# The last chunk's rows of the first sample go straight into y, and y lies in the filters' place

## The chip, the cores and the metric

The kernel runs on one core of one Trainium2 chip. The metric is the device time of one execution in microseconds (us); lower is better. TensorE is called PE, VectorE DVE, ScalarE ACT, GpSimd POOL and SyncE SP, as in the profile. SP does no arithmetic here: it issues DMA transfers, in its program's order, and an issue that waits for a semaphore holds up all issues behind it. POOL and ACT can issue transfers too.

## What is computed

Two layers of a network on x of shape (16, 128, 32, 32): 16 samples, 128 channels, 1024 places. Each layer is a mixer and a feed-forward part, both with a residual. What matters here is the feed-forward part of the first layer and what follows it:

```python
x = x + _L0_conv_ref(_ln_c(x), ...)          # linear attention
t = _to_tokens(x)
t = t + _L0_ffn_ref(_ln_t(t), ...)           # spectral filters: long causal convolutions by FFT,
x = _from_tokens(t, x)                       #   16 filters, two signs, a 128x128 matrix for each
x = x + _L1_conv_ref(_ln_c(x), ...)          # two 3x3 convolutions with batch norm and ReLU
t = _to_tokens(x)
t = t + _L1_ffn_ref(_ln_t(t), ...)           # 64 experts, each token block routed
x = _from_tokens(t, x)
```

The long convolution is a product in the frequency domain: a transform of each sample, at each frequency a product with a 128x128 matrix that is summed over the filters, and an inverse transform.

## The kernel before

It has three stages that follow each other, and the change lies where the second hands over to the third.

**Stage 1, attention and forward transform** (to about 378 us). Sample by sample; the spectra go to DRAM (`vd`), the samples to DRAM (`xd`). DVE mixes the filters' matrices into `mst` (16 KB in each partition), in pieces of 8 of 32 rows.

**Stage 2, products by frequency** (378 to 653 us). The frequencies are cut into `NCH` = 16 chunks of `P / NCH` = 8 rows. For chunk c, PE forms the matrices (`generate`, L816, from `mst` and `ph`), DVE and ACT copy them (`collect`, L827 and L829), and PE multiplies all 16 samples by them (`multiply`, L840). `combine` (L869, L870) and `finish` (L854 to L857) put the results into `ys`, whose partitions are (row in a group of 4, real or imaginary part, sample), so that one chunk of one sample lies in a few partitions only. `finish` then stores `ys` to DRAM as `yd` with two transfers of 512 KB (L861, on SP). The rows of the last two chunks, 14 and 15, have a tensor of their own, `yd[1]` of 16 rows; the other 112 rows are `yd[0]`. `finish` of chunk 15 runs on DVE, of the others on POOL.

**Stage 3, inverse transform, convolutions and routing** (from 653 us; the experts from about 1130 us). `load(b)` (L1032, L1035) fetches sample b: `xd[b]` into `xp`, 512 KB, and its frequencies into `y`, which has two buffers: 112 rows of `yd[0]` (896 KB) and 16 rows of `yd[1]` (128 KB). For sample 0, `xp` and the 112 rows come on POOL's queue, the 16 rows on SP's; for all others everything comes on SP's queue. POOL (L1048 to L1057) and DVE (L1061 to L1078) form `z` from `y`, PE multiplies both with `wi` (L1132, the inverse transform), DVE adds the sample (L1139), and so on through the first convolution: ACT copies the image (L1182, L1189), DVE forms `abss` (L1198), POOL writes `v` from it (L1202), and PE convolves (L1012).

The order of stage 3 on PE, DVE, ACT, POOL and SP is written out ahead of time by a planner that interleaves samples; each engine runs its instructions strictly in that order. At its start the samples 0, 1 and 2 overlap: on DVE and POOL the `z` of sample 2 stands ahead of the first convolution's `abss` and `v` of sample 0. The tensors of the convolution weights (`cw`, twice 1152 KB) and small biases are loaded on SP between sample 1 and sample 2. Each transfer on SP uses one of eight semaphores in turn, so it also waits for the transfer eight before it on those.

So that PE doesn't stand still during the handover, `keep(ps, "cv", 26)` puts 26 products on it whose results nobody reads (L164; each is recorded as two matmuls).

Buffers of a stage lie where those of the stage before lay. `mst` is in the pool `lconst`, which ends with stage 2; the `y` buffers are in the pool `first` of stage 3.

Of the kernel before, what the change touches and what calls it, by code (L numbers as in the profile page):

```python
# [8 lines left out]
F32 = mybir.dt.float32  # L9
AF = mybir.ActivationFunctionType  # L10
ALU = mybir.AluOpType
# [3 lines left out]
P = 128  # L15
B, C, H, W = 16, 128, 32, 32
# [15 lines left out]
NM = NQ // 2  # L32
NCH = 16
JL = 8
# [6 lines left out]
RG = P // KR  # L41
EPR = P // RG
MB = 8
# [26 lines left out]
def metaformer_kernel(ctx: ExitStack, tc: tile.TileContext, io: dict, out: bass.AP):  # L70
    nc = tc.nc
    xs = io["x"].rearrange("b c h w -> b c (h w)")
    outs = out.rearrange("b c h w -> b c (h w)")

    const = ctx.enter_context(tc.tile_pool(name="const", bufs=1))


    ident = const.tile([P, P], F32, name="ident")
# [97 lines left out]
    with ExitStack() as l0:  # L176
        lconst = l0.enter_context(tc.tile_pool(name="lconst", bufs=1))
# [35 lines left out]
            nc.vector.tensor_tensor(seg[:, i : i + 1], seg[:, i - 1 : i], hard[:, i : i + 1], ALU.add)  # L213
        coef = lconst.tile([P, NF], F32, name="coef")
        nc.vector.tensor_scalar(coef, wmix, sig, None, ALU.mult)
        mst = lconst.tile([P, EPR, C], F32, name="mst")
        ph = lconst.tile([P, NCH, CW], F32, name="ph")


        with ExitStack() as a0:  # L220
# [427 lines left out]
            def filters():  # L648

                wfm = setup.tile([P, NQ // 2, 2 * P], F32, name="wfm", tag="mi")  # L650
                nc.vector.tensor_scalar(wfm, wf[:, 1::2, :], -1.0, None, ALU.mult)

                def values(q, dst):
                    for sgn in range(2):
                        w = wfm[:, q // 2, :] if sgn and q % 2 else wf[:, q, :]
                        nc.tensor.matmul(
                            dst, phi[:, q, sgn, :], w, start=(sgn == 0), stop=(sgn == 1)
                        )

                yield  # L660
                xf = spectrum_tile()
                for parity in range(2):
                    pe = class_values(parity, values)
                    t = class_copy(pe, 1)
                    ts = class_copy(pe, ROT) if parity else t
                    ab = class_sums(parity, pe, t)
                    class_differences(parity, ab, pe, ts)
                    yield
                    for part in range(2):
                        butterflies(ab, xf, parity, part)  # L670
                    if parity:
                        butterflies(ab, xf, 1, butterflies(ab, xf, 1, 2))
                    yield
                half = CW // 2
                e, o = (xf[:, :, i].rearrange("p c r m j -> p c (r m j)") for i in range(2))
                nc.vector.tensor_tensor(ph[:, :, :half], e, o, ALU.add)
                nc.vector.tensor_tensor(ph[:, :, half:], e, o, ALU.subtract)
                for m in range(EPR // MB):
                    es = slice(m * MB, (m + 1) * MB)
                    for i in range(NF):  # L680
                        mi = setup.tile([P, MB, C], F32, name="mi", tag="mi")
                        nc.sync.dma_start(mi, io["M_phi"][i, :, es, :])
                        yield
                        if i == 0:
                            nc.vector.tensor_scalar(mst[:, es, :], mi, coef[:, 0:1], None, ALU.mult)
                        else:
                            nc.vector.scalar_tensor_tensor(
                                mst[:, es, :], mi, coef[:, i : i + 1], mst[:, es, :], ALU.mult, ALU.add
                            )

            def prepare():
# [84 lines left out]
        with ExitStack() as g0:  # L776
# [33 lines left out]
            def generate(c, q):  # L810

                pg = [psg.tile([P, 4, CW], F32, name="pg", tag="p") for r in range(RG)]
                for i in range(4):
                    for r in range(RG):
                        rs = slice(r * KR, (r + 1) * KR)
                        nc.tensor.matmul(  # L816
                            pg[r][:, i], mst[rs, 4 * q + i, :], ph[rs, c, :], start=True, stop=True,
                        )
                return pg

# [28 lines left out]
            def finish(c, ys):  # L849

                eng = nc.gpsimd if c + 1 < NCH else nc.vector
                e = cpl.tile([P, JL // RG, 2, C], F32, name="ye", tag="ye", bufs=1)
                yv = ys[:, :, 0]
                eng.tensor_tensor(e, yv[:, :, :2], yv[:, :, 2:], ALU.add)  # L854
                eng.tensor_tensor(yv[:, :, 2:], yv[:, :, :2], yv[:, :, 2:], ALU.subtract)
                eng.tensor_tensor(yv[:, :, 0], e[:, :, 0], e[:, :, 1], ALU.add)
                eng.tensor_tensor(yv[:, :, 1], e[:, :, 0], e[:, :, 1], ALU.subtract)  # L857
                for kl in range(JL // RG):
                    last = c + 2 >= NCH
                    j0 = kl * RG + (c - NCH + 2 if last else c) * JL  # L860
                    nc.sync.dma_start(  # L861
                        yd[last][j0 : j0 + RG].rearrange("g r b x e -> (g r b) (x e)"),
                        ys[:, kl].rearrange("p x m e -> p (x m e)"),
                    )
# [69 lines left out]
    with ExitStack() as c1:  # L934
# [11 lines left out]
        RING = tuple(f"xp{pr}" for pr in AWAY) + (  # L946
            "y", "wi", "z", "y", "cw0", "v", "cw1", "p1", "yo",
        )
        FIRST = ("wi", "v", "cw0", "cw1", "p1", "y")
        halves = {}  # L950

        def load_half(h):

# [2 lines left out]
            if g >= E // EG:  # L956
                pr = AWAY[0] + h - 2 * (E // EG)
                if pr in AWAY:
                    tag = RING[(pr - AWAY[0] + 18) % len(RING)]
                    pool = first if tag in FIRST else xpool if tag[:2] == "xp" else work  # L960
                    x = pool.tile([P, 2, N], F32, name=f"xb{pr}", tag=tag, bufs=RING.count(tag))
                    for j in range(2):
                        xt[2 * pr + j] = x[:, j]
                        nc.sync.dma_start(x[:, j], xd[2 * pr + j])
                return
            pool = first if tag in FIRST else xpool if tag[:2] == "xp" else work
            w = pool.tile([P, EG * HID], F32, name=f"we{n}", tag=tag, bufs=RING.count(tag))
            if n == 0:
                nc.sync.dma_start(
# [53 lines left out]
        def tokens(t):  # L1023
            return t.rearrange("p (j c) -> p j c", c=C)

        yts, xp = {}, {}

        def load(b):
            if b % 2 == 0:
                xp[b // 2] = xpool.tile([P, 2, N], F32, name=f"xp{b // 2}", tag=f"xp{b // 2}")  # L1030
            xt[b] = xp[b // 2][:, b % 2]
            (nc.sync if b else nc.gpsimd).dma_start(xt[b], xd[b])  # L1032
            yts[b] = first.tile([P, 2, 2 * NM, C], F32, name="y", tag="y", bufs=2)
            for i, js in enumerate((slice(P - 2 * JL), slice(P - 2 * JL, P))):
                (nc.gpsimd if b + i == 0 else nc.sync).dma_start(  # L1035
                    yts[b][js].rearrange("p r x e -> p r (x e)"),
                    yd[i][:, :, b].rearrange("j r x e -> j r (x e)"),
                )


# [456 lines left out]
        with tc.manual_schedule(engines=PINNED | {mybir.EngineType.SP}):  # L1497
# [7 lines left out]
            for j in range(2):  # L1505
                nc.sync.dma_start(b2[j * E : (j + 1) * E, :], w2[:, HID, :])
            samples = [None] * B
            keep(ps, "cv", 26)
            for b, name in order:
                if name == "yin":  # L1510
                    if b > 1:
# [303 lines left out]
```

## Time and profile before

| | us |
|---|---|
| median of 4 runs | 1238.72 (1237.3 to 1244.49) |
| the profiled execution, its own time | 1238.84 |
| its span, first to last instruction | 1237.0 |
| outside the span | 1.84 |
| PE busy in the span | 1162.1 (94%) |
| DVE, ACT, POOL busy | 934.5, 724.9, 603.4 |
| mean granted clock of PE | 0.992 of full speed |

By stretches of the span (busy us of each engine, DMA as the mean busy share of the 16 DMA engines):

| stretch, us | PE | DVE | ACT | POOL | clock | DMA |
|---|---|---|---|---|---|---|
| 396 to 640, stage 2 | 239.44 of 244 | 176.23 | 185.41 | 202.64 | 1.00 | 0.38 |
| 640 to 665, handover | 21.07 of 25 | 8.11 | 3.45 | 9.52 | 0.97 | 0.66 |
| 665 to 700, start of stage 3 | 28.46 of 35 | 20.77 | 12.54 | 12.15 | 0.87 | 0.75 |
| 700 to 1130, stage 3 | 415.83 of 430 | 376.20 | 229.09 | 160.08 | 1.00 | 0.31 |
| 1130 to 1237, experts and output | 91.59 of 107 | 41.59 | 23.96 | 9.44 | 0.95 | 0.90 |

PE's busy time in the handover counts the products of `keep`, so it is not all work. A row of the chain of waits gives start, duration and the step; it is followed back from the last instruction, so work on it is work that something later waited for. In the timeline the brackets at the end of a row give the idle time of the engine before it and who ended that.

### The profile page before, as it was taken

The numbers are of one execution on the slowest core, as the hardware profiler recorded it, in microseconds if no ns is written. First come the engines' busy times: TensorE is split into PE (matmuls) and PEld (weight loads), VectorE is DVE, ScalarE is ACT, GpSimd is POOL, SyncE is SP. The second block draws the span as 40 slices with busy tenths as digits, with TensorE's granted clock in tenths as the row PEclk, the third lists the DMA queues.
The fourth block names the chain that finished last, engine by engine and source line by source line (L and its number), as shares of the span: only waits on it lengthen the run. The fifth ranks groups of instructions, "written<-read, shape, count | busy, mean of one in ns | idle before, by whom it ended". The sixth has DMA issues, their size and how long they took to land.

```text
span 1237.0 us, 34413 instructions
## 1 busy us (share of the span) xinstructions
PE 1162.1 (94%) x14398; PEld 954.8 (77%) x14398; DVE 934.5 (76%) x1944; ACT 724.9 (59%) x1420; POOL 603.4 (49%) x800
## 2 busy tenths in 40 slices
PE   7889999999999999999997899999999999998996
PEld 6667777777767998888887788898888888885453
DVE  5888888888766777777764589898988989885235
ACT  4777787777655777777761345555555555544211
POOL 2435454655568788888882433343343333230003
PEclk9999999999999999999998999999999999999998
DMA  7005334353436334343449522223233321416899
GB/s 281 24 31 168 120 116 154 96 171 101 154 120 180 103 126 139 133 139 132 131 135 288 127 51 52 86 87 120 84 122 118 103 86 69 154 34 223 317 403 384
DMA packets 91243, 175.14 MB, mean 142 GB/s; under 512 B 5968, under 2 KB 42064, under 8 KB 90448
## 3 DMA queue, kind: packets, MB, share of 16 engines
q1 hardware_dynamic: 90448, 170.46, 41.3%
q0 software_dynamic: 640, 2.49, 0.6%
q8 instruction: 113, 1.85, 0.6%
q14 instruction: 42, 0.34, 0.1%
HBM read 110.28 MB, written 62.65 MB: 140 GB/s over the span
## 4 chain that ended last, share of the span: by engine, by line
PE 55%; DVE 22%; issue 11%; ACT 6%; DMA 4%; POOL 1%; SPq 1%; POOLq 0%; ACTq 0%; DVEq 0%
PE pg L816 10%; PE pcv L1012 10%; PE py L840 9%; PE big L638 7%; DVE bst L135 4%; PE big L171 3%; PE big L152 3%; PE big L570 3%; PE big L450 2%; PE big L533 2%; PE big L432 2%; DVE abss L1255 1%; DVE xp L1277 1%; DVE xp L1139 1%; ACT tt L144 1%
## 5 line engine op out<-in xcount | busy, mean ns | idle before, releaser
L1012 PE MATMUL pcv<-v,cw 128*128 128x256 f32 x1152 | 259.9, 382 | 3.5 <-POOL v L1202 3.5
L1012 PEld LDWEIGHTS pcv<-v,cw 128*128 128x128 f32 x1152 | 216.1, 191 | 36.9 <-issue 4.9
L829 ACT COPY g<-pg 128x512 f32<-128x512 f32 x316 | 161.2, 606 | 39.2 <-PE pg L816 38.6
L827 DVE COPY g<-pg 128x512 f32<-128x512 f32 x196 | 127.8, 682 | 70.4 <-PE pg L816 70.4
L816 PE MATMUL pg<-ph,mst 32*128 32x128 f32 x4096 | 144.1, 280 | 5.8 <-issue 4.5
L816 PEld LDWEIGHTS pg<-ph,mst 32*128 32x128 f32 x4096 | 128.6, 186 | 22.2 <-issue 11.8
L840 PE MATMUL py<-g,v 128*32 128x128 f32 x4096 | 124.7, 274 | 1.3 <-POOL v L808 1.3
L840 PEld LDWEIGHTS py<-g,v 128*32 128x32 f32 x4096 | 108.0, 110 | 9.1 <-POOL v L808 1.8
L144 ACT ACTIVATE tok<-tok,sts 128x128 f32<-128x128 f32 x256 | 101.9, 480 | 16.9 <-DVE sts L1089 13.6
L135 DVE BATCH_NORM_STATS2 bst<-big 128x6 f32<-128x256 f32 x256 | 91.2, 418 | 21.1 <-PE big L152 11.7
L807 POOL TENSOR_TENSOR v<-xc 128x256 f32<-128x256 f32 x128 | 99.6, 801 | 13.6 <-DMA xc<-vd 13.3
L638 PE MATMUL big<-u,mu 128*128 128x128 f32 (+4 forms) x384 | 86.0, 380 | 0.0
L1202 POOL TENSOR_TENSOR v<-abss 128x256 f32<-128x256 f32 x64 | 49.1, 787 | 68.1 <-DVE abss L1198 56.7
L286 POOL TENSOR_TENSOR xf<-ab 128x256 f32<-128x256 f32 x34 | 24.8, 728 | 110.4 <-DVE ab L253 110.3
L1221 POOL TENSOR_TENSOR yo<-abss 128x256 f32<-128x256 f32 x32 | 23.5, 734 | 110.3 <-DVE abss L1217 110.3
L638 PEld LDWEIGHTS big<-u,mu 128*128 128x128 f32 x384 | 56.8, 191 | 18.0 <-issue 15.4
L570 PE MATMUL big<-wf,ub 128*128 128x256 f32 x256 | 62.0, 385 | 0.2
L144 ACT ACTIVATE tt<-tt,sts 128x128 f32<-128x128 f32 x128 | 51.1, 481 | 14.6 <-DVE sts L1089 14.6
L808 POOL TENSOR_SCALAR v<-v 128x256 f32<-128x256 f32 x64 | 55.2, 863 | 5.6
L475 POOL TENSOR_TENSOR ke<-ke,ks 128x1024 f32<-128x1024 f32 x16 | 30.6, 1913 | 55.1 <-DVE qs L483 43.5
L570 PEld LDWEIGHTS big<-wf,ub 128*128 128x128 f32 x256 | 46.2, 190 | 8.7 <-ACT xn L423 3.0
L914 ACT COPY yt<-py 128x512 f32<-128x512 f32 x60 | 35.1, 585 | 28.0 <-ACT g L829 18.0
(256 smaller groups left out, 2488.6 us busy)
## 6 DMA issues: line engine op xcount, KB each, us to landing
we<-in_weight SPq DMA_DIRECT2D x32, 1024.0 KB, 9.2
xc<-vd SPq DMA_DIRECT2D x64, 256.0 KB, 3.3
yd<-ys SPq DMA_DIRECT2D x32, 512.0 KB, 3.5
vd<-xf SPq DMA_DIRECT2D x15, 1024.0 KB, 5.1
y<-yd SPq DMA_DIRECT2D x15, 896.0 KB, 6.6
x<-in_x SPq DMA_DIRECT2D x16, 512.0 KB, 5.0
mi<-in_M_phi SPq DMA_DIRECT2D x16, 512.0 KB, 4.6
xd<-x SPq DMA_DIRECT2D x16, 512.0 KB, 6.3
```

Source lines behind the costliest of these rows:

```text
L135: nc.vector.bn_stats(bst[:, j : j + 2, :].rearrange("p j s -> p (j s)"), src[:, j : j + 2, :].rearrange("p j c -> p c j"),)
L144: nc.scalar.activation(dst[:, j, :], src[:, j, :], AF.Identity, bias=nm[:, j : j + 1], scale=r[:, j : j + 1],)
L570: nc.tensor.matmul(dst, self.ub[:, q, :], wf[:, q, :], start=True, stop=True)
L638: nc.tensor.matmul(self.pa[:, a:hi], mu[:, NF - 1 - si, tap, :], self.u[:, a - tap : hi - tap], start=(tap == 0), stop=(tap == KU - 1),)
L807: nc.gpsimd.tensor_tensor(vv[:, x, 1:, bs], e, o, op)
L808: nc.gpsimd.tensor_scalar(v[:, :, 0, bs], v[:, :, 2, bs], -1.0, None, ALU.mult)
L816: nc.tensor.matmul(pg[r][:, i], mst[rs, 4 * q + i, :], ph[rs, c, :], start=True, stop=True,)
L827: nc.vector.tensor_copy(dst, src)
L829: nc.scalar.copy(dst, src)
L840: nc.tensor.matmul(py[rows, x, kl, :], v[:, (x * NM + m) * JL + jl, 1 - ri : 3 - ri, :] .rearrange("p k b -> p (k b)"), g[:, ((x * 2 + ri) ...
L1012: nc.tensor.matmul(pc[:, i], wt[:, dy, k, :], v[:, k, dy * WT : dy * WT + HT], start=(dy == 0), stop=(dy == 2),)
L1202: nc.gpsimd.tensor_tensor(v[:, k, WT : WT + HT], self.ab[:, 0], self.ab[:, 1], op)
```

## The change

Three things, in the text below with the parts that only follow from them left out.

- **A short way for 8 of sample 0's rows.** `finish` of chunk 15 first copies sample 0's part of `ys` straight into `y` of sample 0: four transfers from SBUF to SBUF, each of 4 partitions and 16 KB, two issued by SP and two by ACT. Only then it issues its two stores to `yd`. `load(0)` now fetches 112 rows and the 8 rows of chunk 14, both on POOL's queue. `load(1)` and later fetch 112 and 16 rows on SP as before.
- **`y` in the filters' place.** A new pool, `ypool`, lies outside all stages and has two buffers of 8 KB in each partition under the tag "y". In stages 1 and 2 they hold `mst`, now two tiles of 16 rows each; in stage 3 they hold `y`. The pool `first` no longer holds `y`, so its other tiles lie at other addresses.
- **A shorter stopgap on PE.** `keep(ps, "cv", 26)` becomes `keep(ps, "cv", 13)`.

```diff
+    ypool = ctx.enter_context(tc.tile_pool(name="ypool", bufs=2, reuse_waits="tile"))
+    def y_tile(b):
+        if b not in yts:
+            yts[b] = ypool.tile([P, 2, 2 * NM, C], F32, name="y", tag="y", bufs=2)
+        return yts[b]
...
-        mst = lconst.tile([P, EPR, C], F32, name="mst")
+        mst = [
+            ypool.tile([P, EPR // 2, C], F32, name=f"mst{i}", tag="y", bufs=2) for i in range(2)
+        ]
+        def mrow(i, n=1):
+            h, k = divmod(i, EPR // 2)
+            return mst[h][:, k : k + n]
...
                 eng.tensor_tensor(yv[:, :, 1], e[:, :, 0], e[:, :, 1], ALU.subtract)
+                for kl in range(JL // RG if c + 1 == NCH else 0):
+                    for r in range(2):
+                        j0 = P - JL + kl * RG
+                        (nc.scalar if kl else nc.sync).dma_start(
+                            y_tile(0)[j0 : j0 + RG, r].rearrange("p x e -> p (x e)"),
+                            ys[r * B :: 2 * B, kl].rearrange("p x m e -> p (x m e)"),
+                        )
                 for kl in range(JL // RG):
                     last = c + 2 >= NCH
...
             (nc.sync if b else nc.gpsimd).dma_start(xt[b], xd[b])
-            yts[b] = first.tile([P, 2, 2 * NM, C], F32, name="y", tag="y", bufs=2)
-            for i, js in enumerate((slice(P - 2 * JL), slice(P - 2 * JL, P))):
-                (nc.gpsimd if b + i == 0 else nc.sync).dma_start(
-                    yts[b][js].rearrange("p r x e -> p r (x e)"),
-                    yd[i][:, :, b].rearrange("j r x e -> j r (x e)"),
+            n = JL if b else 0
+            for i, js in enumerate((slice(P - 2 * JL), slice(P - 2 * JL, P - JL + n))):
+                (nc.sync if b else nc.gpsimd).dma_start(
+                    y_tile(b)[js].rearrange("p r x e -> p r (x e)"),
+                    yd[i][: js.stop - (js.start or 0), :, b].rearrange("j r x e -> j r (x e)"),
                 )
...
-            keep(ps, "cv", 26)
+            keep(ps, "cv", 13)
```

With the planner's order unchanged, the order of instructions on each engine differs only here: SP issues two small transfers between the stores of chunk 14 and those of chunk 15, and no longer one of 16 rows behind them; ACT issues two small transfers after its last copy of stage 2; POOL issues one more load, of 8 rows, behind the 112; PE has 13 products fewer. The filters' products are the same, from two tiles.

## The prediction

> **What bounds the kernel now.** I read the busy time by stretches first. The change can only act where stage 2 hands over to stage 3, so I then took the chain of waits there; its lines from 652 to 691 us are these.
>
> ```profile
> 652.54 0.34 DVE ys L857
> ...
> 652.90 0.32 SPq L861
> ...
> 653.27 6.98 DMA yd<-ys
> ...
> 660.69 0.63 SPq L1035
> ...
> 663.27 10.31 DMA cw<-cwd
> ...
> 673.59 12.18 DMA y<-yd
> ...
> 685.87 0.43 DVE z L1061
> ...
> 688.89 0.61 DVE abss L1198
> ...
> 689.56 0.73 POOL v L1202
> ```
>
> The chain is not what one expects. It goes from the last result (DVE, 652.88) to its store, which lands at 660.24, to SP's row of issues from 660.69 on, and then not through sample 0 at all: it stays in the DMA queue, through `cw` and the load of `y` of sample 2, which lands at 685.8. Only there does it return to an engine. In the timeline this is seen from the engines' side.
>
> ```profile
> 664.18 0.43 DVE L1061 TENSOR_TENSOR z<-y 128x256 f32<-128x256 f32 x1 [11.30 <-DMA y<-yd]
> ...
> 683.02 1.02 ACT L1189 COPY p<-big 128x1024 f32<-128x1024 f32 x1
> ...
> 685.87 0.43 DVE L1061 TENSOR_TENSOR z<-y 128x256 f32<-128x256 f32 x1 [5.94 <-DMA y<-yd]
> ```
>
> DVE waits 11.30 us for `y` of sample 0 and later 5.94 us for `y` of sample 2. Behind the second wait stands `abss` of sample 0 (688.81), whose input, ACT's copy L1189, was done at 684.04. So sample 0 was ready 4.77 us before it could go on: a head start of sample 0 alone would only lengthen that wait. What sets the end here is when the DMA queue reaches `y` of sample 2. The table by stretches of 2 us shows that queue (the last two columns are DMA share and GB/s; ahead of them the granted clock).
>
> ```profile
> 654.00:656.00 2.00, 2.00 (x12) 1.74 (x11) 0.00 (x0) 0.00 (x0) 0.00 (x0) 1.00 1.04 330
> 656.00:658.00 2.00, 2.00 (x11) 1.77 (x10) 0.00 (x0) 0.00 (x0) 0.00 (x0) 1.00 1.01 393
> 658.00:660.00 2.00, 2.00 (x11) 1.77 (x10) 0.00 (x0) 0.00 (x0) 0.00 (x0) 1.00 0.48 197
> 660.00:662.00 2.00, 0.91 (x5) 0.46 (x3) 0.00 (x0) 0.00 (x0) 0.00 (x0) 1.00 0.01 4
> 662.00:664.00 2.00, 0.00 (x0) 0.00 (x0) 0.00 (x0) 0.00 (x0) 0.00 (x0) 0.89 0.69 238
> 664.00:666.00 2.00, 1.67 (x8) 1.70 (x9) 1.78 (x3) 0.00 (x0) 1.75 (x2) 0.50 1.03 342
> ```
>
> The DMA engines are full to 658, all but empty to 662.6, and full again to 690. They are empty because SP stands still from 653.7 to 660.69: its next issue, the last 16 rows of sample 0, waits for the store, and everything for the later samples stands behind it.
>
> **The change, part by part.** The sum is made against the profiled execution, 1238.84 us (span 1237.0 and 1.84 outside), 0.12 above the median.
>
> First, sample 0. Removed is the way over DRAM: store (landed 660.24), issue 0.63, landing 3.4 us after the issue, 664.1. Added are four transfers of 16 KB from 652.9 on. An issue of SP on such tiles took 0.32 to 0.44 us (the four stores, L861), so SP's second leaves at about 653.3 and ACT's likewise. Nothing in the trace is an SBUF to SBUF transfer; the smallest there, `gb` with 0.2 KB, landed after 2.4 us, the 128 KB load after 3.4. That puts them at 655.7 to 656.7. The later bound for `y` of sample 0 is POOL's queue: the 112 rows, issued at 648.36, landed after 9.9 us, 658.3. The 8 rows of chunk 14 wait for that chunk's stores (issued 647.83, landing 5.1 later, 652.9), are 64 KB, and come behind the 112 rows; I put `y` at 658.6. Its bounds: 658.3, and 662.8 if the 8 rows take the 9.9 us of their predecessor from 652.9. Sample 0 then starts 5.5 us earlier (1.3 in the slow case). On POOL only `z` stands behind the added issue, which takes about 0.7 us (the 112-row issue, 0.69); on ACT, idle for 25.49 us until 675.46, nothing does.
>
> The Trainium skill speaks against splitting: DMA: Bandwidth & Descriptors, Bandwidth, asks for about 1 MiB a transfer and calls those under 64 KB dominated by descriptors. By that page's fit (Anatomy of one DMA), about 2.0 us fixed for each, an estimate of mine for two on one queue without any overlap is 4.0 us, which the sum would not feel.
>
> Second, SP's queue, where the gain is. No wait for the store remains ahead of sample 1's `xp` and its 112 rows: they need only chunk 14's stores (652.9), so they are issued from about 654.3, against 661.38 and 661.99. The stores of chunk 15 go out some 0.7 us later (two issues), but the DMA engines are busy then with POOL's loads. The wait for the last store (about 660.9) now stands ahead of sample 1's 16 rows; `cw`, the biases and sample 2 are queued behind it. At that time most of sample 1's 1.4 MB still lies in the queue, at 300 GB/s (between the rows' 289 and 342 at 664 to 668) up to 4.7 us of work, so it doesn't run dry before `cw` follows. What is saved is the empty time: (1 - 0.48) x 2 + (1 - 0.01) x 2 + (1 - 0.69) x 2 = 3.64 us. A second hole, 668 to 670 with a share of 0.88, comes from the same late start (SP waits for sample 1's landing until 670.70) and gives 0.24. Bytes don't change: 4 x 16 KB and 64 KB for 128 KB. `y` of sample 2 lands 3.9 us earlier, 681.9. Its other conditions are met: its buffer is free when POOL has read sample 0, 667.78 - 5.5 = 662.3, and its queue slot when sample 1's last rows have landed, about 667.
>
> Third, what is late next. `z` of sample 2 ends 2.9 us after its landing (685.87 to 688.81), at 684.9; sample 0's input is ready at 684.04 - 5.5 = 678.5, or 682.7 in the slow case. Sample 1's `y` lands at about 671.0 - 3.9 = 667.1 (its last rows, issued at 662.62, took 8.4), where `z` of it would like to start at 671.47 - 5.5 = 666.0; that costs sample 0 about 1 us of a slack of 6. So the whole 3.9 goes on to `abss`, `v` and PE's convolution (690.34 to 686.4). From there the trace has no wait for a load of `y`: the queue is empty at 691 and SP waits for DVE, 44.7 us in all to 760. So the shift is kept; the expert weights at the end are issued behind computed results and move along.
>
> Fourth, PE's stopgap: 13 fewer products, 26 matmuls of 11.49 / 52 = 0.221 us, end at 655.2 for 660.9. PE idles from there to `y`, about 3.4 us; before it was 3.42 (660.91 to 664.33), and the clock was 0.50 from 664 to 670. I expect the same clock. If the cover is gone and the clock falls sooner, sample 0's first products run slow as they do now, under the same slack: nothing. Products of no use don't set the end.
>
> A rule from the skill belongs here: TensorE: Matmul & The Clock Gate, What's actually happening, has the clock halved after an idle window of about 3.4 us that runs freely, so a gap of this length may or may not fall. By the rule sample 0 may run at full clock, which the sum again doesn't feel.
>
> Fifth, the filters' place. Products and copies are the same in number and order. `wi` now waits for chunk 14's last product, which ended at about 641.8; it was issued at 642.14, so that is free. `y` of both samples needs the filters' last product, 639.8, long past. Zero.
>
> Sum: 1238.84 - 3.9 = 1234.9 us, or 0.31% less.
>
> **The rivals.** One: *sample 0 sets the pace.* If the queue gains more than I think, the end follows sample 0's 5.5 us: 1233.3. If on top PE's gap ahead of the convolution (3.47 us at 690.34) goes, its 24 matmuls take 5.18 us, as warm ones do in the chain, for 7.13: 1.95 more, 1231.4. For it: the head start is real. Against it: the chain doesn't pass through sample 0. Chance 0.17.
>
> Two: *the queue is not refilled.* Sample 1's loads share the engines with stores and POOL's loads, these land later by what the others gain, and SP waits for them as before. The gain is then 0 to 1.5: 1238 or so. For it: 1.04 and 1.01 of DMA share at 654 to 658, no room there. Against it: the hole after 658 is there, and loads wait to fill it. Chance 0.09.
>
> Three, on the other side: *POOL's load is starved.* SP's queue never runs empty now; if POOL's queue were served only when it does, `y` of sample 0 would come after `cw` (the second, issued at 663.9, landed after 12.7, 676.6), at about 676.6 - 3.9 = 672.7. It decides from 668.9 on (664.1 plus the slack of 4.77); from there each us costs one: 672.7 - 668.9 = 3.8, 1242.6. Against it: from 649 to 660 the DMA table has 1.44 MB on POOL's queue and 1.96 MB on SP's, side by side. Chance 0.06.
>
> Four: *it doesn't do what it says*, some transfer waiting where I see none; about 0 either way, 1238.8. Chance 0.04.
>
> **How the numbers follow.** My forecast has 0.64: a gain of 2.5 to 6. A measurement of this kernel can tell about 0.5% from no change, 6.2 us, that is 1232.5 and 1244.9. The forecast, rivals two and four, and most of one lie inside: 0.78. Faster by more needs the clock's part of one and the best of the forecast: 0.16. Slower by more needs starvation to 675.1 or something unseen: 0.06. The range reaches from the better end of one, 1231.4, to 1239.5, which is rivals two and four with 0.7 for scatter (three of the four runs lie within 1.5); outside are the last of one and all of three.
>
> **What would show it.** Right: DMA share near 1 from 658 to 664; `y` of sample 0 used at about 658.6 and DVE's wait 11.30 down to about 5.8; DVE's wait for `y` of sample 2 still there, no shorter than 5.94, ending near 682; the convolution at 686.4; from 700 on the same rows, 4 us earlier. Wrong: no wait for `y` of sample 2 (then one), a hole in the DMA share at 660 (two), or `z` of sample 0 after 664 (three).

## The result, and the profile after

The changed kernel is slower, by a little: 1242.28 us median of 47 runs (1236.65 to 1249.48) against 1237.81 of 73 runs of before (1232.1 to 1247.01); the ratio is 1.0035, 95% interval 1.0025 to 1.0045. That is about 4.4 us, inside the 0.5% that the prediction said could not be told from no change, but above its range of 1231.4 to 1239.5, and on the other side of before. The profiled execution took 1239.90 us (span 1238.0), 1.06 above that of before, so it is one of the better ones; single executions of either kernel lie some 3 us around their median. Three executions among the runs below took 1303, 6330 and 6540 us and count in no median or ratio.

The handover first. DVE's and POOL's rows of the timeline; the brackets give the idle time before a row and who ended it.

```profile
658.11 0.58 POOL L1060 DMA_DIRECT2D y<-yd  x1 [9.59 <-DMA yd<-ys]
668.51 0.42 DVE L1086 TENSOR_TENSOR z<-y 128x256 f32<-128x256 f32 x1 [15.20 <-DMA y<-yd]
684.74 0.43 DVE L1086 TENSOR_TENSOR z<-y 128x256 f32<-128x256 f32 x1 [1.07 <-DMA y<-yd]
```

Sample 0 is not used at 658.6 but at 668.5, 4.3 us later than before: POOL's load of the 8 rows could only be issued at 658.11, when the second store of chunk 14 had landed, and then took 10.3 us for 64 KB, beside sample 1's loads on SP's queue. DVE's wait for `y` of sample 2 is nearly gone (5.94 before), and yet sample 2 starts only 1.1 us earlier. The table by stretches (granted clock, DMA share and GB/s at the end of a row) shows the hole filled as foreseen, but with slow traffic: share 1 and no more than 187 to 313 GB/s, where the same time before held a hole and then 342.

```profile
658.00:660.00 2.00, 0.00 (x0) 0.00 (x0) 0.00 (x0) 0.00 (x0) 0.58 (x1) 0.96 1.00 313
660.00:662.00 2.00, 0.00 (x0) 0.00 (x0) 0.00 (x0) 0.00 (x0) 0.00 (x0) 0.50 0.98 299
662.00:664.00 2.00, 0.00 (x0) 0.00 (x0) 0.00 (x0) 0.00 (x0) 0.00 (x0) 0.50 1.03 258
664.00:666.00 2.00, 0.00 (x0) 0.00 (x0) 0.00 (x0) 0.00 (x0) 0.00 (x0) 0.50 1.10 214
666.00:668.00 2.00, 0.00 (x0) 0.00 (x0) 0.00 (x0) 0.00 (x0) 0.00 (x0) 0.50 1.02 187
```

The loss is not there. From stage 2's last result to sample 0's residual (DVE L1277, now L1302) the handover is 2.1 us shorter than before (74.7 for 76.8 us), and everything from sample 3 on is 1.7 us early. All of it and more is lost in the last 40 us, where the change touches nothing. PE's rows of the timeline there, before and then after: the products of the last experts, eight transposes, and the stopgap of four products; the last row is SP's issue of the last store.

```profile
1205.97 1.08 PE L1588 MATMUL peo<-we,ht 128*32 128x128 f32 x32 [0.68 <-DVE ht L1579]
1208.15 1.09 PE L1625 MATMUL big<-ident,ot 128*128 128x128 f32 x8 [0.36 <-DVE ot L1600]
1209.08 1.89 PE L164 MATMUL wm<-ident 128*128 128x256 f32 x8
...
1231.26 1.14 SPq L1659 DMA_DIRECT2D out<-xp  x1
```

```profile
1203.73 1.08 PE L1613 MATMUL peo<-we,ht 128*32 128x128 f32 x32 [1.48 <-DMA we<-in_weight]
1205.90 1.94 PE L1650 MATMUL big<-ident,ot 128*128 128x128 f32 x8 [0.36 <-DVE ot L1625]
1207.63 2.76 PE L172 MATMUL wm<-ident 128*128 128x256 f32 x8
...
1230.78 1.14 SPq L1684 DMA_DIRECT2D out<-xp  x1
```

Before, the last products wait for DVE; after, for their weights, 1.48 us. The clock is then halved (0.50 from 1206 to 1208, in the table by stretches), and transposes and stopgap take 4.70 us for 2.98. From the start of the last store's issue the span goes on for 7.2 us (1230.78 to 1238.0), before for 5.8 (1231.26 to 1237.0). I call *tail* the time from the start of DVE's third last copy into `ot` to the end of the span: 33.5 us before, 37.5 after. Of the 4.0 us more, 0.8 is the longer wait, 1.7 the half clock and 1.4 lies behind the last store's issue. The sum of the pair: stage 2's end +0.4, handover -2.1, from there to the experts -1.4 (before has 3.4 us of half clock at 1134.6, after has none there), tail +4.0; together 0.9, the difference of the spans is 0.96.

### The profile page after: what moved, and what is told of

The parts are those of the page before. It is cut to its first block, busy times and chain, and to the rows that moved or that the text cites. A ratio compares the mean times of both kernels' runs of the same rounds, so it can differ in the third digit from the quotient of the medians.

```text
span 1238.0 us, 34372 instructions
## 1 busy us (share of the span) xinstructions
PE 1153.8 (93%) x14372; PEld 949.7 (77%) x14372; DVE 935.4 (76%) x1944; ACT 724.9 (59%) x1420; POOL 604.2 (49%) x801
## 3 DMA queue, kind: packets, MB, share of 16 engines
q8 instruction: 113, 1.85, 0.6%
## 5 line engine op out<-in xcount | busy, mean ns | idle before, releaser
L844 ACT COPY g<-pg 128x512 f32<-128x512 f32 x316 | 161.1, 606 | 36.8 <-PE pg L831 35.8
```

Source lines behind the costliest of these rows:

```text
L844: nc.scalar.copy(dst, src)
```

## The experiments

All ratios are to the runs of before that were taken with them, with 95% intervals. The kernels of the table are described below it. The theories: one, late rows (POOL's load holds sample 0); two, cold PE (the halved stopgap lets the clock fall at the handover); three, the place (other addresses of `y` and `mst`); four, the weights of the last experts come late against PE, and this goes with PE's shorter stream of instructions; five, which came out of four: it is where the pieces of PE's code lie.

| kernel | loads | products, more than before | ratio | last experts wait | 8 transposes | tail |
|---|---|---|---|---|---|---|
| before | old | 0 | | 0.68 | 1.09 | 33.5 |
| after | new | -13 | 1.0035 (1.0025 to 1.0045) | 1.48 | 1.94 | 37.5 |
| again | new | -13 | 1.0059 (1.0037 to 1.0082) | 2.68 | 1.97 | 38.0 |
| direct2 | new, all direct | -13 | 1.0036 (1.0020 to 1.0052) | 3.13 | 1.97 | 38.8 |
| gap13_old | old | -13 | 1.0037 (1.0017 to 1.0058) | 2.91 | 1.97 | 39.7 |
| wide13 | new | -13 | 1.0032 (1.0012 to 1.0053) | 3.21 | 1.97 | 40.6 |
| phase51 | old | +51 | 1.0058 (1.0032 to 1.0084) | 1.10 | 1.97 | 37.2 |
| place_only | old | 0 | 1.0003 (0.9987 to 1.0019) | 0.89 | 1.09 | 33.9 |
| keep26 | new | 0 | 1.0026 (1.0013 to 1.0039) | 0.95 | 1.09 | 34.2 |
| narrow26 | new | 0 | 1.0012 (0.9991 to 1.0033) | | | |
| direct2_26 | new, all direct | 0 | 1.0013 (0.9995 to 1.0031) | 0.85 | 1.09 | 33.9 |
| act_tail | old, refilled | 0 | 0.9996 (0.9984 to 1.0009) | 0.67 | 1.09 | 33.5 |
| held26 | new, held | 0 | 0.9997 (0.9980 to 1.0013) | 0.95 | 1.09 | 34.3 |
| phase64 | old | +64 | 1.0022 (1.0000 to 1.0043) | 0.90 | 1.09 | 33.7 |
| phase13 | old | +13 | 0.9999 (0.9981 to 1.0016) | 0.77 | 1.09 | 33.6 |
| phase32 | old | +32 | 1.0006 (0.9990 to 1.0021) | 0.68 | 1.09 | 33.5 |
| after_phase13 | new | +13 | 0.9991 (0.9975 to 1.0007) | 0.83 | 1.66 | 35.8 |
| wf_after | new, weights first | -13 | 1.0026 (1.0007 to 1.0045) | 0.67 | 1.09 | 34.8 |
| wf_before | old, weights first | 0 | 0.9995 (0.9976 to 1.0013) | 0.67 | 1.09 | 33.5 |
| wf_after_p13 | new, weights first | +13 | 1.0002 (0.9984 to 1.0020) | 0.68 | 1.09 | 34.0 |

The last three columns are of one profile each, in us: PE's wait ahead of the last experts' products, the time of the eight transposes behind them (1.09 at full clock), and the tail. The profile of narrow26 is of the execution of 6330 us and is not read; that of phase51 is of the one of 1303 us, and only the pattern is read from it. The other 18 profiles are called "the 18" below.

keep26 needs a word ahead: with the new loads and the count of before it is still 0.26% above before, clear of 1. The rows with the new loads and the count of before average 1.0017 (keep26, narrow26, direct2_26; held26, with its changed order, is at 0.9997), so the new loads brought nothing, and whether they cost something is not told apart.

### The changed kernel once more, and its parts

The changed kernel again, without an edit:

> The changed kernel once more, for a second profile. The first one puts sample 0 at 668.5 us (4.3 later than before), z of sample 2 1.1 earlier, everything from sample 3 on 1.7 earlier, and loses 2.7 after that, in the last 40 us. Theory one, late rows (the 64 KB of chunk 14 on POOL's queue, 10.3 us, hold sample 0): z of sample 0 again at 667 to 670; if they land later still, z of sample 2 no longer comes first and the whole time follows. Theory two, cold PE (13 us of idle ahead of sample 0 after half the stopgap): a granted clock below before's 0.87 from 665 to 700. Theory three, the place (y and mst in other addresses): loss outside 640 to 700. The loss of the last 40 us comes again only by theory three; otherwise it is scatter. All three expect 1240 to 1244 us, 2.5 to 6 above before.

The two profiles of one kernel differ at the handover. In this one the stores of chunk 14 had landed at 654.4, the 8 rows took 3.3 us, and sample 0 came 9.1 us earlier than in the first profile:

```profile
654.97 0.58 POOL L1060 DMA_DIRECT2D y<-yd  x1 [6.80 <-DMA yd<-ys]
659.40 0.42 DVE L1086 TENSOR_TENSOR z<-y 128x256 f32<-128x256 f32 x1 [4.26 <-DMA y<-ys]
```

The tail is long again (38.0 us), which was said to be scatter unless theory three holds. So late rows come and go, and the tail's loss stays: theory one can't be the cause of that loss.

The place alone: the new pool and the two tiles of `mst`, with the old loads and 26 products.

```diff
-            keep(ps, "cv", 13)
+            keep(ps, "cv", 26)
...
-                for kl in range(JL // RG if c + 1 == NCH else 0):
...
-            n = JL if b else 0
...
```

> Before, with y and mst in the shared place and nothing else (old loads, 26 products of stopgap). Theory three: 3 to 5 us slower than before, about 1241 to 1243. Theories one and two, and the prediction's fifth step: within 0.7 us of before, sample 0 at 664 as before.

1.0003: theory three falls. The stopgap of before in the changed kernel:

```diff
-            keep(ps, "cv", 13)
+            keep(ps, "cv", 26)
```

> After, with 26 products of stopgap instead of 13: PE stands still from about 658.5 instead of 655.8 until y of sample 0. Theory two: better than after by 2 us or more, 1238 to 1240, with the clock from 665 to 700 above 0.88. Theory one: as after within 0.7 us, because the wait for the rows of chunk 14 remains at about 10 us of idle time, sample 0 at 667 to 670.

1239.45 for 1242.96 of again, on the same chip; the tail is 34.2 and the half clock behind the last experts is gone. So the stopgap matters, as theory two says, though in the profile the gain lies 540 us later than theory two has it. The rows of chunk 14 also straight into `y`:

```diff
-                for kl in range(JL // RG if c + 1 == NCH else 0):
+                for kl in range(JL // RG if c + 2 >= NCH else 0):
...
-                        j0 = P - JL + kl * RG
-                        (nc.scalar if kl else nc.sync).dma_start(
+                        j0 = P - (NCH - c) * JL + kl * RG
+                        (nc.scalar if kl and c + 1 == NCH else nc.sync).dma_start(
...
```

> After, with the rows of chunk 14 going straight from its results into y as well (four more transfers of 16 KB on SP ahead of its stores), so that POOL's queue has no load of 8 rows and waits for no store. Theory one: sample 0 at 657.5 to 660 instead of 668.5, DVE's wait ahead of it 15.2 down to 5 to 7, time 3 to 8 us below after, that is 1234.5 to 1239. Theory two: PE's idle time falls from 13 us to 2 to 4 as well, so it expects the same and the clock from 665 to 700 above 0.90. Theory three: no better than after, 1241 to 1243, for the place is the same.

Sample 0 is early for certain now, and it brings nothing: 1241.24, the tail 38.8.

```profile
660.32 0.43 DVE L1085 TENSOR_TENSOR z<-y 128x256 f32<-128x256 f32 x1 [6.69 <-DMA yd<-ys]
```

### Cover or number of instructions

The stopgap has two sides: how long PE is kept, and how many instructions stand in its stream. These four part them. The old loads with 13 products, as an edit of place_only:

```diff
-            keep(ps, "cv", 26)
+            keep(ps, "cv", 13)
```

> Before's loads and order, y in the shared place (1.0003 of before by itself), and 13 products of stopgap instead of 26: of the change only the shorter stopgap. Theory two, cold PE: PE idles from about 655 to 664, 6 us more than before; slower than before by 1 to 3 us. Theory four, the weights' lag: in the changed kernel the weights of the last experts land about 2 us later against PE than before (PE stands at 1203 to 1206, then the clock falls to half for 3.4 us), and it goes with the 26 instructions fewer in PE's stream: slower than before by 3 to 5 us, with a clock below 0.9 from 1200 to 1212. Theory one, late rows: as before, within 0.7 us.

13 products of 512 columns:

```diff
-            wm = ps.tile([P, 2, P], F32, name="wm", tag=tag, bufs={"s": 2, "cv": 3}[tag])
+            wm = ps.tile([P, cols, P], F32, name="wm", tag=tag, bufs={"s": 2, "cv": 3}[tag])
...
-            keep(ps, "cv", 13)
+            keep(ps, "cv", 13, 4)
```

> After, with 13 products of 512 columns instead of 256 as stopgap: PE is kept as long as by 26 (to about 661) with the number of instructions of 13. Theory two: as with 26 of them, 1238 to 1240. Theory four: as after, 1241 to 1244, clock below 0.9 from 1200 to 1212.

26 products of 128 columns, by the same new argument:

```diff
-            keep(ps, "cv", 13)
+            keep(ps, "cv", 26, 1)
```

> After, with 26 products of 128 columns instead of 13 of 256: PE is kept no longer than in after (to about 656) with the number of instructions of before. Theory two: as after, 1241 to 1244. Theory four: as with 26 full ones, 1238 to 1240, no clock below 0.9 from 1200 to 1212.

direct2 with 26 products:

```diff
-            keep(ps, "cv", 13)
+            keep(ps, "cv", 26)
```

> The rows of both last chunks straight into y, with 26 products of stopgap. With 13 it took 1241.2. Theories two and four: 3 us less than that or more, 1235 to 1238, and last weights no later against PE than before. Theory one: as with 13, 1240 to 1242.

gap13_old is as slow as the whole change, 1.0037, and nothing of the change is in it but the place and 13 products fewer. wide13 covers the handover as before did (its stopgap ends 8.0 us after stage 2's last result, as before's) and is slow, 1.0032, with a tail of 40.6: theory two falls. narrow26, whose columns are no more than after's, is at 1.0012 and not told from before; on the same chip its median is 3.0 us under wide13's, but the two intervals overlap. Theory four stands, by the tails above all: in the nine profiles up to here they are 37.5 us or more at 13 products and 34.2 or less at 26, whatever the cover and the loads. gap13_old's rows at the end:

```profile
1206.93 1.08 PE L1605 MATMUL peo<-we,ht 128*32 128x128 f32 x32 [2.91 <-DMA we<-in_weight]
1209.25 1.97 PE L1642 MATMUL big<-ident,ot 128*128 128x128 f32 x8 [0.36 <-DVE ot L1617]
1211.01 3.62 PE L172 MATMUL wm<-ident 128*128 128x256 f32 x8
```

Its table by stretches there, with the granted clock third from the end:

```profile
1208.00:1210.00 2.00, 1.24 (x7) 0.94 (x6) 0.56 (x2) 0.00 (x0) 0.00 (x0) 0.50 1.04 422
1210.00:1212.00 2.00, 2.00 (x9) 1.82 (x8) 0.67 (x3) 0.00 (x0) 0.00 (x0) 0.50 1.02 414
```

And wide13's and direct2_26's last products, the one with the count of after, the other with that of before:

```profile
1210.95 1.15 PE L1613 MATMUL peo<-we,ht 128*32 128x128 f32 x32 [3.21 <-DMA we<-in_weight]
```

```profile
1209.70 1.08 PE L1612 MATMUL peo<-we,ht 128*32 128x128 f32 x32 [0.85 <-DVE ot L1624]
```

### Fewer instructions, or other places of the pieces

The table of DMA queues of before's page has a row for code:

```profile
PE 1162.1 (94%) x14398; PEld 954.8 (77%) x14398; DVE 934.5 (76%) x1944; ACT 724.9 (59%) x1420; POOL 603.4 (49%) x800
...
q8 instruction: 113, 1.85, 0.6%
```

113 pieces of 1.85 MB together, 16 KB each, for 2 x 14398 records of PE (matmuls and weight loads): one piece for 255 records. A product of the stopgap is 4 records, so 64 products are one piece, and 13 fewer move every later piece by 52 records against the work. The Trainium skill (Runtime: NRT & Kernel Launch, Instruction fetch mechanics) has the same unit, blocks of 16 KiB or 256 instructions that the sequencer fetches by DMA while it works, and calls the price of a boundary mostly hidden; the runs below are about that last word. If places count, 51 products more must be as bad as 13 fewer, and 64 more as good as none. With before's loads:

```diff
-    def keep(ps, tag, count):
+    def keep(ps, tag, count, tiny=0):
...
+        for _ in range(tiny):
+            nc.tensor.matmul(wm[:32, 0, :8], ident[:32, :32], ident[:32, :8], start=True, stop=True)
...
-            keep(ps, "cv", 26)
+            keep(ps, "cv", 13, 64)
```

> Before, with 13 full products of stopgap and 64 tiny ones (32x32 weights, 8 columns): 77 products in place of 26, so 51 more, PE kept to about 660 to 664. In the trace PE's code comes in pieces of 16 KB, one for 256 records, and a product is 4 records, so 51 more put the later pieces where 13 fewer do (51 + 13 = 64 products = 256 records). Theory five, the place of the pieces: slower than before by 3 to 6 us, last experts waiting for weights and the clock halved near 1207, as with 13 fewer. Theory four in its plain form (fewer instructions are worse) and theory two: as before, within 1 us.

The control, by the same argument:

```diff
-            keep(ps, "cv", 26)
+            keep(ps, "cv", 13, 77)
```

> The control: 13 full and 77 tiny products, 64 more than before, so that the later pieces of code start at the same instructions as in before. Theory five: as before, within 1 us, no half clock near 1207. If the tiny products cost time by themselves (they end near 664 to 666), it is 1 to 2 us slower, as the other one then is too.

Two other places, 13 and 32 in two kernels:

```diff
-            keep(ps, "cv", 26)
+            keep(ps, "cv", 26, 13)   # or 32
```

> Before, with 26 full products and 13 tiny ones: pieces of code start 52 records earlier in the later work than in before. Theory five says only that it may differ: anything from 2 us better to 5 us worse, the difference in the last 40 us. Theories two and four (plain): as before, within 1 us.

> Before, with 26 full products and 32 tiny ones: pieces of code start 128 records, half a piece, earlier. Theory five: may differ, 2 us better to 5 us worse, in the last 40 us. Theories two and four (plain): as before, within 1 us.

phase51 has more instructions than before and is slow by 0.58%, with the halved clock behind the last experts. phase64 has the tail of before (33.7 us) and no half clock there:

```profile
1207.34 1.08 PE L1590 MATMUL peo<-we,ht 128*32 128x128 f32 x32 [0.90 <-DVE ot L1602]
```

It is still 0.22% slower (interval from 1.0000); its tiny products fill PE to 664.6, when `y` of sample 0 is there already; whether they cost it that was not told apart. The intervals of phase51 and phase64 overlap too, so what sets them apart is the tail, and phase51's is of its long execution. phase13 and phase32 are as before. So "fewer is worse" falls, and theory five fits all rows: -13 and +51 are the same place, and have tails of 37 to 41 us, against 33.5 to 34.3 in all eight profiles at 0 or +64, and 33.5 and 33.6 in the two of old loads at +32 and +13. (wf_after, below, has another order of loads at the end.)

### Where the 3.9 us of the refilled queue went

The refill alone: before, with the last rows of sample 0 on ACT's queue.

```diff
-                (nc.gpsimd if b + i == 0 else nc.sync).dma_start(
+                (nc.sync if b else nc.scalar if i else nc.gpsimd).dma_start(
```

> Before, with one load moved: the last 16 rows of sample 0, which wait for the last stores, go on ACT's queue, so that SP's queue goes on with sample 1 at once. This is the refill alone, stopgap 26. The prediction's second step: y of sample 2 at 30 us after the last result of stage 2 instead of 33.3, and 2 to 4 us less time, 1233 to 1235. If the refill delays sample 0's rows (they share the DMA engines now) beyond its slack, or the pace is not set there: as before within 1.5 us, with sample 0 used 13 to 20 us after the last result instead of 11.7.

The new way of sample 0 alone: after, 26 products, sample 1's last rows ahead of its other loads.

```diff
+            if b == 1:
+                rows(1, slice(P - 2 * JL, P))
             (nc.sync if b else nc.gpsimd).dma_start(xt[b], xd[b])
+            rows(0, slice(P - 2 * JL))
+            if b != 1:
+                rows(1, slice(P - 2 * JL, P - JL + n))
```

> After, with 26 products of stopgap, and sample 1's last 16 rows ahead of its other loads on SP's queue, so that the queue stands until the last stores have landed, as before. This is the new way of sample 0 alone. The prediction: no gain without the refill, 1237 to 1238.5, y of sample 2 at 33 us after the last result. If the refill is what costs in the changed kernel: better than its 1239.5. If the new way of sample 0 costs: as that, 1238.5 to 1240.

The changed loads at a harmless place of the pieces:

```diff
-            keep(ps, "cv", 13)
+            keep(ps, "cv", 26, 13)
```

> After, with 26 full and 13 tiny products of stopgap: the pieces of PE's code lie as in the kernel of old loads that took 0.9999 of before. Theory five: no half clock near 1207, and the last 33.5 us as before. If the changed loads gain as predicted: 1233 to 1235. If they are worth nothing or less, as the runs with 26 say: 1237 to 1240.

act_tail fills the queue and is as before, 0.9996. DVE uses `y` of sample 2 from 30.2 us after stage 2's end for 33.0, and no longer waits for it, but sample 0 comes later, its rows now beside sample 1's loads:

```profile
669.00 0.43 DVE L1061 TENSOR_TENSOR z<-y 128x256 f32<-128x256 f32 x1 [15.47 <-DMA y<-yd]
```

held26 is as before too, 0.9997, and so is after_phase13, 0.9991, though its profile begins the tail 7.3 us ahead of before. 2.3 us of that are lost in the tail, where its clock fell too:

```profile
1198.84 1.08 PE L1615 MATMUL peo<-we,ht 128*32 128x128 f32 x32 [0.83 <-DVE ot L1627]
...
1201.01 1.66 PE L1652 MATMUL big<-ident,ot 128*128 128x128 f32 x8 [0.36 <-DVE ot L1627]
```

### The late weights by themselves

The last half of the experts' weights is issued ahead of two loads of `xb` that stood before it.

```diff
-                    load_half(2 * g + len(RING))
+                    if 2 * g + len(RING) != 2 * ng:
+                        load_half(2 * g + len(RING))
...
                     load_half(2 * g - 1 + len(RING))
+                    if 2 * g + len(RING) == 2 * ng:
+                        load_half(2 * ng)
```

> After (13 products, its new loads), with one exchange at the end: the last half of the experts' weights is issued ahead of the two loads of xb (2 x 512 KB, about 2.5 us of queue) that stood before it. If the late weights are the loss: the last products wait about 0.7 us instead of 1.5 to 3.1, no half clock near 1207, and 3 to 5 us less time, 1236.5 to 1239 for 1242 to 1243. If the lateness is only beside it: 1241 to 1243.

> Before, with the same exchange. Its last products wait 0.68 us, 0.4 of it not for weights, so there is little to gain: 0 to 1 us less, 1236 to 1238, the last 33.5 us unchanged.

> After with 26 full and 13 tiny products (0.9991 of before) and the same exchange. Late weights as the loss: without the half clock that one profile of it showed near 1201, 0 to 2 us better than without the exchange, 1234.5 to 1237, 0.05 to 0.3% under before. If the changed loads are worth nothing: as before within 1 us.

In wf_after the wait and the half clock are gone, as expected, and the tail is 34.8:

```profile
1209.52 1.08 PE L1613 MATMUL peo<-we,ht 128*32 128x128 f32 x32 [0.67 <-DVE ht L1604]
1211.70 1.09 PE L1653 MATMUL big<-ident,ot 128*128 128x128 f32 x8 [0.36 <-DVE ot L1625]
```

So the late weights and the half clock are 2.7 us of the tail. What is left of its growth, 1.3 us, lies behind the last store's issue, 7.1 us from the end there as in after. That the time gains as much is not shown: it is 1.0026, and the intervals of after and wf_after overlap. wf_before has nothing to gain and gains nothing. wf_after_p13, the version that the runs pointed to, had sample 0's residual earlier than any other profile (723.3 us) and a short tail (1232.57 us in all) but is as before over its runs, 1.0002. No version beat before by more than can be measured.

## Why the prediction was wrong

**The step that failed** is first the fourth, the stopgap: "nothing". It looked for the price where the products stand, and found cover for every us of it. wide13 shows that the number of instructions costs with the cover of before too. The trace of before had the row of code pieces, and I did not ask what 52 records fewer move. Averaged over the table (wf_after, which undoes part of it, left out), the six rows at -13 and +51 lie at 1.0043, the eight at 0 or +64 at 1.0008: a difference of 0.35%, 4.3 us, as much as the result. The tails differ by 4.7 us: 38.6 us on the mean of the six, 33.9 of the seven others that have a profile that is read. Within the new loads alone the difference is less, 1.0041 for the four rows at -13 and 1.0017 for keep26, narrow26 and direct2_26: 0.24%, 3 us of the 4.4.

That is a third to a half of the way from the forecast, 0.9968 of before, to 1.0035. The rest is the second step's gain of 3.9 us, which did not reach the end: with the stopgap at 0 or +13 the new loads should have shown it, and keep26, narrow26, direct2_26 and after_phase13 lie at 1.0011 on the mean. By these figures either alone would have left the time at 1238 to 1239 us, inside the range; the two together did not.

**First step, sample 0.** 658.6 was right in the second profile (659.4) and wrong in the first (668.5). The term that was mis-sized is the landing of chunk 14's stores: I took 5.1 us, the middle of 3.4 and 6.9, where the load needs the later one; it came at 654.4 and at 657.5. The issues were also dearer than said: 0.5 to 1.1 us each of the four small ones for 0.32 to 0.44, so that sample 1's first load left SP 2.7 us after stage 2's end in both profiles, where I had 1.4. The upper bound of 9.9 us for the load was the right one for the first profile (10.3). Rival three had this mechanism and its point, 668.9; the first profile stops 0.4 us short of it.

**Second step, the refill.** The mechanism holds: in the chain of waits of the second profile the work still goes over the last store, SP's issue of sample 1's rows, `cw` and `y` of sample 2, but with 0.86 us of issues between the store's landing and `cw` instead of 3.03.

```profile
657.40 4.43 DMA yd<-ys
...
661.90 0.60 SPq L1060
...
662.69 9.58 DMA cw<-cwd
672.26 0.02 issue
672.28 11.60 DMA y<-yd
```

The size is off. Over the profiles of both kinds of loads (nine new, seven old, with act_tail and held26 left out), DVE uses sample 2 from 30.1 us after stage 2's end with the new and 31.3 with the old, 1.2 us instead of 3.9. Two things in the profiles can have taken the rest. The hole was priced by its share of busy DMA time, and in the first profile it was filled with traffic at 187 to 313 GB/s. And the hole of before's profile is not always there: in 9 of the 18 profiles PE stood still for 1.2 to 2.4 us between 645 and 653 (below), stage 2 ended at 653.5 to 659.3 instead of 651.3 to 654.1 while POOL's loads went on, and the last stores could land sooner; in gap13_old they landed 4.9 us after stage 2's end instead of 7.4. In those profiles the new loads are no faster (handovers of 72.5 to 75.3 us against 71.7 to 74.8); in the others they are (72.0 to 74.7 against 74.2 to 77.0). That the gain is confined to the undelayed half is read from these profiles, not tried.

**Third step, what is late next.** Right: sample 0's residual follows sample 2's first use by 42.1 to 45.1 us in each of the 18 profiles, whatever the loads. That the shift is then kept to the end was wrong in part: in the kernels at -13 the last weights don't move with it, and after_phase13, 7.3 us ahead at the last experts of its profile, is no faster over its runs than can be measured.

**Fifth step, the place.** Right, place_only is 1.0003. **The rivals:** none of them was the cause; all four looked at the handover. The chance of 0.78 for a difference of less than 0.5% covered the result, the range did not.

**Open:** why pieces at these places make the last weights late. What the traces show is this. Each transfer has sixteen completions, and its landing is the last one. For the weights from 1190 to 1200 the last completion comes 1.5 to 2.0 us after the first at 0, +13, +32 and +64, and 2.2, 3.0, 3.8, 3.5, 4.0 us at -13 (after, again, direct2, gap13_old, wide13; 2.4 in wf_after), with the same bytes moved by then (direct2 and place_only: 15.2 MB left at 1196 in both). The last stores have it too: 0.9 to 1.4 us from the first completion to the last at -13, wf_after among them, against 0.2 in all others; that is the time behind the last store's issue. The lag starts in the transfer that is issued at 1152 before (1149 after): 0.3 to 1.0 us there in all others, 2.3 to 3.3 at -13. In all six profiles at -13 a piece of code sets out 0.1 to 0.3 us before the last two loads of the gates (at 1146 in after) and is on its way beside them for 0.7 to 1.1 us. In the eight at 0 and +64 it sets out 0.8 to 1.3 us before them and is done by then or at most 0.3 us later; at +13 and +32 no piece is within 2 us of their start. phase51's profile speaks for it only in part: the piece lies as at -13 and the last weights lag by 3.2 us, but the lag starts in a later transfer. That this neighbour is the cause is argued from these times, not shown.

## What to carry to other kernels

Work that nobody needs is still in the stream of instructions: adding or removing some moves every later piece of that engine's code, and here, where the DMA queues are full at the end and PE runs within a us of its data, 13 products of no use went with 3 to 4 us at the end. So before a small difference is put down to the edit, run it once with the same count of instructions and once with the same cover; and look at where two runs part in time, not only at the place of the change. An empty stretch of a DMA queue in one profile is an estimate of what can be won there only if other executions show it too.

## What the hardware showed that was not expected

PE seems to run out of code. In 9 of the 18 profiles, of kernels with and without the change, it stands between 645 and 653 with nothing that the profile shows as its releaser; in the second profile of the changed kernel:

```profile
648.33 3.47 PE L855 MATMUL py<-g,v 128*32 128x128 f32 x115 [2.00 <-issue]
```

There a piece came at 645.9, 7.1 us after the one before it; in the first profile, without the stop, they came 3.2 to 5.4 us apart (635.5, 638.7, 644.1, 647.6). In all nine profiles with the stop, the piece next to it came 5.9 to 7.9 us after the one before; in the nine others no two pieces from 636 to 652 lie more than 5.4 us apart. That the late piece stops PE is read from these times, not tried. It can be one source of the scatter of some 3 us between executions.

The granted clock fell to one half for 3.41 us or 2, 3 or 4 times that, in all of the 18 profiles but for the last stretch, which the end of the work cuts; the falls of one trace lie whole multiples of 3413 ns apart, to 3 ns. The Trainium skill (TensorE: Matmul & The Clock Gate, What's actually happening) gives a window of 3413 ns that runs freely, which fits these lengths and that after_phase13 fell after a wait of 0.83 us at the last experts, where keep26, at 0.95, did not. With windows laid on the falls of each trace, PE was busy for 1.82 us of the window ahead of that fall, and for 0.9 to 1.8 in all seven profiles with a fall there, phase51's among them; in the twelve without, no window there had less than 1.97. So no idle window was needed for it, as the prediction had it from the skill. Nor does the busy time decide alone: in wide13 the clock held after a window with 1.4 us, at 652.

A copy from SBUF to SBUF of 16 KB has no landing of its own in the rows; the second profile bounds it: `y` was complete 2.6 us after the last of the four issues had ended (656.84 to 659.40), 4.2 us after the first had begun (655.17) and 4.3 after the last result. The prediction had 2.8 to 3.8 from the last result; its estimate of 4.0 us for two on one queue, without overlap, is near the 4.2, though the fit behind it is for transfers that GpSimd issues and these four are SP's and ACT's.
